# AdaLN block with a scan: one weight matrix laid out with its input features in partitions, its row norms summed on TensorE

## The chip, the cores and the metric

The kernel runs on one core of a Trainium2 chip. The metric is the device time of one execution in microseconds (us), as the median of several runs. The program is compiled from a hand-written order: each of the five engines (PE = TensorE, DVE = VectorE, ACT = ScalarE, POOL = GpSimd, SP = SyncE, which here only issues DMAs) works through its own queue strictly in order and waits on semaphores for the others.

## The reference, cut to what matters

```python
mod = (silu(c) @ wmod).reshape(2, 6, 1, 512)          # sa, ca, ga, sb, cb, gb
h = layernorm(x) * (1 + ca) + sa                      # x: 2 x 4096 x 512
xn = h / norm(h) * sqrt(512) * gamma
q, kv, a = split(einsum('bnd,ed->bne', xn, W_qkva), 3)   # W_qkva: 1536 x 512
a = sigmoid(a)
y_t = a_t * y_{t-1} + kv_t                            # scan along the 4096 rows
x = x + ga * (q * y)
h = layernorm(x) * (1 + cb) + sb
x = x + gb * fp4_linear(silu(fp4_linear(h, w_gate)) * fp4_linear(h, w_up), w_down)
```

`fp4_linear` quantizes both operands in blocks of 16. All inputs and the output are f32. Only the first product, with `W_qkva`, and what prepares it is touched here. To keep f32 accuracy the kernel splits each operand of that product into two f16 parts, "hi" and "lo", and sums three products (hi·hi, hi·lo, lo·hi). Every row of `W_qkva` times gamma is first scaled by the reciprocal of its norm, and the scale is multiplied back behind the product.

## The kernel before, in words

**Stages.** The first stage (attention) takes up about the first 580 us, the second (the feed-forward network) the rest. The attention stage is a loop over `slot` = 0 to 63 and three more. Slot `4*i + e` computes block `i` (512 rows of x) against group `e` (128 features of each of the three parts q, kv, a): `mix` issues 3 parts x 4 input chunks x 3 passes = 36 matmuls of 128x128 by 128x512. In slot 0 the block is cut into four quarters of 128 rows, so that each quarter can start when its own rows are there.

**What a slot needs.** (1) The rows of x: 128-row tile `g` is loaded (`norm_load`), its moments taken on DVE (`norm_moments`, `norm_stats`, two small POOL operations), centred and shifted on DVE (`norm_center`, `norm_shift`), squared on ACT with a sum (`norm_square`), turned into a reciprocal norm by two small POOL operations (`norm_gain`), scaled to f16 on ACT (`norm_hi`), its remainder formed on DVE (`norm_lo`), and both halves are transposed by a DMA on SP's queue into `xT`. Tiles 0 to 3 are prepared in `start`; tile `slot + 4` is finished in each slot, so slot 4 can begin when tile 7 has been transposed. (2) The weights of group `e`. Before, a piece of `W_qkva` arrives with its 128 *output* features in partitions. It is multiplied by gamma (DVE, L281), squared and summed on ACT (`square_qkva`, L285), its scale computed (`inverse_qkva`, a DVE operation and a POOL power, L288 and L289), split into hi (ACT or DVE, L308 and L310) and lo (DVE, L316), and transposed by a DMA on SP's queue (L324): twelve pieces, three for each group. Groups 0 and 1, and most of 2, are made in `start`, group 3 in slots 0 and 1. (3) The PSUM banks of two slots earlier read out.

**Behind each product**, one slot later: `gates` (ACT sigmoid), `scan` (DVE), `read_out` (DVE), `halves` (ACT copy, DMA transpose), then `joined` (ACT) and `residual` (POOL add, POOL's DMA).

**The opening** also computes the modulation rows on PE: `mod_spread(1, 0)` and `mod_spread(0, 0)` (each four f32 products, spread over all partitions, copied to `ca[0]` and `sa[0]`), `mod_rows` twice, and `mod_columns(2)` behind slot 0. Their weights `wmod` come in 256 KB loads.

**What sets the order.** `order = tc.manual_schedule(...)`: every engine's queue, SP's included, is the order of the Python calls. The SP queue carries all loads and all DMA transposes; a DMA reuses one of eight semaphores and therefore also waits for the DMA issued eight places earlier.

Of the kernel before, what the change touches and what calls it, by code (L numbers as in the profile page):

```python
# [6 lines left out]

# [36 lines left out]
def tile_adaln_block(  # L44
# [150 lines left out]
    wq = {divmod(n, 3): piece(2, n, 1) if n < 11 else piece(1, 2 * KC, 1) for n in range(12)}  # L195

    cT = atile([P, KC, B], F32, "cT")
    sc = atile([P, KC, B], F32, "sc")
    with nc.allow_non_contiguous_dma(reason="c is 4 KB"):
        for b in range(B):  # L200
            S.dma_start(cT[:, :, b], c[b].rearrange("(k p) -> p k", p=P))
# [4 lines left out]

    def load_part(e, part):
        S.dma_start(wq[e, part], w_qkva[part * D + e * P : part * D + (e + 1) * P, :])
# [61 lines left out]
    gam = ctile([P, D], F32, "gam", tag="mod_gb")  # L270
    wqT = atile([P, 2 * KC, 3 * D], F16, "wqT")
    us = atile([P, KC, 3], F32, "us")
    rs = atile([P, KC, 3], F32, "rs")
    gq = atile([P, KC, B], F32, "gq")

    def load_qkva(e):
        for part in (2, 1, 0):
            load_part(e, part)

    def gamma_qkva(e, part, engine=G):  # L280
        engine.tensor_tensor(wq[e, part], wq[e, part], gam, ALU.mult)  # L281

    def square_qkva(e, part):
        sq = work.tile([P, D], BF16, name="sq", tag="sq", bufs=1)
        A.activation(sq, wq[e, part], AF.Square, accum_out=us[:, e, part : part + 1])  # L285

    def inverse_qkva(e, a=0, b=3):
        V.tensor_scalar(rs[:, e, a:b], us[:, e, a:b], 1e-36, 2.0**-28, ALU.max, ALU.mult)  # L288
        G.tensor_tensor(rs[:, e, a:b], rs[:, e, a:b], mhalf[:, : b - a], ALU.pow)  # L289

    def scale_qkva(e):
        inverse_qkva(e)
        gain_qkva(e)

    def gain_qkva(e):
        V.tensor_scalar(
            us[:, e, :], us[:, e, :], 1e-36, 2.0**-28 / (XGAIN * XGAIN), ALU.max, ALU.mult
        )
        G.tensor_tensor(us[:, e, :], us[:, e, :], phalf[:, :3], ALU.pow)

    whl = {}

    def hi_qkva(e, part, on_act):
        w = wq[e, part]
        hl = whl[e, part] = new_hl()
        rsc = rs[:, e, part : part + 1]
        if on_act:
            A.activation(hl[:, 0, :], w, AF.Copy, scale=rsc)  # L308
        else:
            V.tensor_scalar(hl[:, 0, :], w, rsc, None, ALU.mult)  # L310

    def lo_qkva(e, part):
        w = wq[e, part]
        hl = whl.pop((e, part))
        r = part * KC + e
        V.scalar_tensor_tensor(  # L316
            out=hl[:, 1, :],
            in0=w,
            scalar=rs[:, e, part : part + 1],
            in1=hl[:, 0, :],  # L320
            op0=ALU.mult,
            op1=ALU.subtract,
        )
        S.dma_start_transpose(wqT[:, :, r * P : (r + 1) * P], flat(hl))  # L324
# [22 lines left out]
    def norm_shift(g):  # L347
        shift(xh[g], xstat.pop(g)[1], sa[g * P // N])
# [35 lines left out]
    def mix(i, xT, e):  # L384
        ps = [bank(3 * (e % 2) + j) for j in range(3)]
        width = P if i == 0 and e == 0 else TB
        for t in range(0, TB, width):
            for pp, part in zip(ps, PARTS):
                r = part * KC + e
                n = 0  # L390
                for k in range(KC):
                    for wp, xp in PASSES:
                        T.matmul(  # L393
                            pp[:, t : t + width],
                            wqT[:, wp * KC + k, r * P : (r + 1) * P],
                            xT[:, xp * KC + k, t : t + width],
                            start=n == 0,
                            stop=n == 3 * KC - 1,
                        )
                        n += 1  # L400
        return i, e, ps
# [245 lines left out]
    def start():  # L647
        a, b_, c_ = PARTS

        def load_mod_piece(s, k):  # L650
            S.dma_start(wm[s][:, k, :], wmod[k * P : (k + 1) * P, s * D : (s + 1) * D])

        load_mod(1, KC)
        norm_load(0)
        S.dma_start(gam, gamma.partition_broadcast(P))
        for k, then in enumerate((PARTS[0], PARTS[1], PARTS[2], None)):
            if then is None:
                norm_load(1)
            else:
                load_part(0, then)  # L660
            load_mod_piece(0, k)
# [3 lines left out]
        norm_load(KC)  # L665
        pc = mod_spread(1, 0)
        ps = mod_spread(0, 0)
        r1 = mod_rows(1)
        r0 = mod_rows(0)

        norm_moments(0)
        norm_stats(0)
        gamma_qkva(0, a, V)
        A.activation(ca[0], pc, AF.Copy, bias=1.0)
        square_qkva(0, a)
        gamma_qkva(0, b_, V)
        square_qkva(0, b_)
        inverse_qkva(0, a, a + 1)
        norm_center(0)
        gamma_qkva(0, c_, V)  # L680
        inverse_qkva(0, b_, b_ + 1)
        hi_qkva(0, a, True)
        square_qkva(0, c_)
        lo_qkva(0, a)
        inverse_qkva(0, c_, c_ + 1)
        hi_qkva(0, b_, True)
        norm_moments(1)
        norm_stats(1)
        lo_qkva(0, b_)
        A.copy(sa[0], ps)  # L690
        norm_center(1)
        hi_qkva(0, c_, True)
        norm_shift(0)
        norm_square(0)
        lo_qkva(0, c_)
        norm_gain(0, G)
        norm_shift(1)
        norm_square(1)
        norm_hi(0)
        norm_moments(2)  # L700
        norm_moments(3)
        norm_gain(1, G)
        norm_stats(2)
        norm_hi(1)
        norm_stats(3)
        norm_lo(0, xT)
        load_mod_piece(2, 0)
        norm_center(2)
        norm_shift(2)
        norm_square(2)  # L710
        norm_lo(1, xT)
        load_mod_piece(2, 1)
        load_part(2, a)
        norm_gain(2, G)
        norm_center(3)
        norm_shift(3)
        norm_square(3)
        norm_gain(3, G)
        norm_hi(2)
        gamma_qkva(1, a, V)  # L720
        norm_lo(2, xT)
        load_mod_piece(2, 2)
        load_part(2, b_)
        norm_hi(3)
        gamma_qkva(1, b_, V)
        square_qkva(1, a)
        square_qkva(1, b_)
        norm_lo(3, xT)
        load_mod_piece(2, 3)
        load_part(2, c_)  # L730
        norm_load(KC + 1)
        inverse_qkva(1, b_, a + 1)
        gamma_qkva(1, c_, V)
        mod_store(*r1, tag="yh")
        square_qkva(1, c_)
        mod_store(*r0)
        hi_qkva(1, a, False)
        inverse_qkva(1, c_, c_ + 1)
        lo_qkva(1, a)
        hi_qkva(1, b_, True)  # L740
        norm_moments(KC)
        hi_qkva(1, c_, True)
        lo_qkva(1, b_)
        gamma_qkva(2, a, V)
        square_qkva(2, a)
        norm_stats(KC)
        lo_qkva(1, c_)
        norm_load(KC + 2)
        load_qkva(3)
        norm_center(KC)  # L750
        gamma_qkva(2, b_, V)
        square_qkva(2, b_)
# [3 lines left out]
        gamma_qkva(2, c_, V)  # L756
        square_qkva(2, c_)
        gain_qkva(0)
        norm_moments(KC + 1)
        inverse_qkva(2)  # L760
        norm_stats(KC + 1)
        for part in PARTS:
            hi_qkva(2, part, False)
            lo_qkva(2, part)
        gain_qkva(1)
        gain_qkva(2)

# [7 lines left out]
    with order:  # L775
        xT = new_xT()
        start()
        for slot in range(NS + 3):
# [9 lines left out]
            cur = mix(i, xT, e) if slot < NS else None  # L788
# [12 lines left out]
            if slot == 1:  # L801
                for part in PARTS:
                    square_qkva(3, part)
# [7 lines left out]
            if gate is not None:  # L811
                gate = read_out(*gate)
            if g < NT:
# [15 lines left out]
            if slot == 1:  # L829
                scale_qkva(3)  # L830
                for part in PARTS:
                    hi_qkva(3, part, False)
# [228 lines left out]
```

## Time and profile before

| | us |
|---|---|
| median of 3 runs | 1935.84 (1935.71 to 1936.38) |
| time of the profiled execution | 1934.53 |
| its span in the profile | 1932.8 |
| PE busy in the span | 1905.7 (99%) |
| DVE / ACT / POOL busy | 1605.6 / 991.0 / 415.2 |
| attention product L393, 2412 matmuls | 505.2 |
| feed-forward products L888 (two lines) and L935 | 487.7 + 487.7 + 465.8 |

The chain that ended last is PE for 87% of the span. A busy PE is a PE with a matmul in flight; a wait shows as idle time with what released it. The profile's `PEclk` is the TensorE clock that was granted, in shares of full speed. `L393 PE MATMUL mm<-xT,wqT` reads: line 393, engine PE, writes tile `mm`, reads `xT` and `wqT`.

### The profile page before, as it was taken

The page shows a single profiled execution, that of the slowest core. Times are in us where ns is not written, and L with a number is a line of the kernel's source. Part 1 is how long each engine was busy: PE and PEld are TensorE (multiplying, and loading weights), DVE is VectorE, ACT ScalarE, POOL GpSimd, SP SyncE. Part 2 cuts the span into 40 slices and gives each one's busy share as a digit, 9 for nine tenths or more (in the row PEclk, how much of TensorE's full clock was granted, in tenths as well). Part 3 has the DMA queues.
Part 4 walks back from the last instruction along what each step waited for, and adds up shares of the span by engine and source line. Part 5 has one row for each costly group of instructions (what it writes and reads, how often), then busy time and mean ns, then how long its engine had stood idle before and what let it go on. Part 6 is the DMA issues. An engine that isn't in the chain of part 4 may idle for free.

```text
span 1932.8 us, 25689 instructions
## 1 busy us (share of the span) xinstructions
PE 1905.7 (99%) x9220; PEld 899.6 (47%) x9220; DVE 1605.6 (83%) x2677; ACT 991.0 (51%) x1705; POOL 415.2 (21%) x597
## 2 busy tenths in 40 slices
PE   7899999999999999999999999999999999999999
PEld 4344444444444444444444444444444444444444
DVE  6777789999859988888888888878888888888875
ACT  4544467777755544444444444444544454444432
POOL 4544466666520100000000100001000000000000
PEclk9999999999999999999999999999999999999999
DMA  9787689999933444334433443344434333433343
GB/s 234 182 233 189 165 184 201 220 202 202 188 85 60 87 72 80 69 63 76 79 66 63 78 80 74 63 82 81 63 63 82 76 63 66 81 74 63 63 68 58
DMA packets 483201, 206.67 MB, mean 107 GB/s; under 512 B 439622, under 2 KB 440902, under 8 KB 483072
## 3 DMA queue, kind: packets, MB, share of 16 engines
q1 hardware_dynamic: 468624, 171.50, 41.8%
q0 software_dynamic: 14448, 33.52, 10.0%
q8 instruction: 72, 1.18, 0.3%
q14 instruction: 57, 0.47, 0.1%
HBM read 63.12 MB, written 33.58 MB: 50 GB/s over the span
## 4 chain that ended last, share of the span: by engine, by line
PE 87%; DVE 0%; issue 0%; ACT 0%; POOL 0%; ACTq 0%
PE mm L888 47%; PE sd L935 24%; PE mm L393 16%; ACT y L435 0%; DVE o L953 0%; DVE o L964 0%; DVE ld L172 0%; DVE st L153 0%; DVE hl L372 0%; DVE y L420 0%; DVE ld L166 0%; DVE hid L908 0%; ACT sig L405 0%; ACT sq L354 0%; DVE inv L100 0%
## 5 line engine op out<-in xcount | busy, mean ns | idle before, releaser
L888 PEld LDWEIGHTS <-x2T 128*128 128x128 f16 x4608 | 450.9, 98 | 469.4 <-issue 1.3
L393 PE MATMUL mm<-xT,wqT 128*128 128x512 f16 (+1 forms) x2412 | 505.2, 373 | 15.0 <-DMA xT<-hl 8.0
L888 PE MATMUL mm<-wuT,x2T 128*128 128x512 f16 (+1 forms) x2304 | 487.7, 361 | 1.0 <-DVE hid L908 1.0
L888 PE MATMUL mm<-wgT,x2T 128*128 128x512 f16 (+1 forms) x2304 | 487.7, 361 | 0.0
L935 PE MATMUL sd<-wdT,hT 128*128 128x512 f16 x2112 | 465.8, 379 | 0.0
L393 PEld LDWEIGHTS <-wqT 128*128 128x128 f16 x2412 | 231.9, 99 | 289.8 <-issue 22.0
L935 PEld LDWEIGHTS <-hT 128*128 128x128 f16 x2112 | 206.7, 98 | 242.7
L903 ACT ACTIVATE silu<-mm,u 128x512 f32<-128x512 f32 (+1 forms) x192 | 124.6, 650 | 285.7 <-PE mm L888 281.9
L908 DVE SCALAR_TENSOR_TENSOR hid<-mm,u,silu 128x512 f32<-128x512 f32 (+1 forms) x192 | 128.6, 673 | 139.8 <-PE mm L888 130.7
L590 POOL TENSOR_SCALAR rstd<-vs 128x1 f32<-128x1 f32 x64 | 14.9, 232 | 982.8 <-ACT sq L588 982.8
L143 ACT ACTIVATE u<-ud,rms 128x1 f32<-128x1 f32 x64 | 18.9, 295 | 278.3 <-DVE rms L139 278.3
L120 ACT ACTIVATE sle<-sl 128x512 f16<-128x512 f32 (+2 forms) x162 | 146.9, 907 | 0.0
L113 ACT ACTIVATE she<-sh 128x1408 bf16<-128x1408 bf16 (+1 forms) x128 | 128.3, 1003 | 4.1
L959 POOL DMA_DIRECT2D out_dram<-o x63 | 56.2, 892 | 270.2 <-DVE o L953 266.4
L411 DVE TENSOR_TENSOR_SCAN y<-sig,cy,mm 128x512 f32<-128x512 f32 x56 | 71.7, 1280 | 45.8 <-ACT sig L405 17.3
L427 ACT COPY yh<-y 128x1024 uint16<-128x1024 uint16 x64 | 66.9, 1046 | 79.6 <-DVE y L420 76.5
L122 DVE SCALAR_TENSOR_TENSOR xn<-hid,xn 128x1408 f32<-128x1408 f32 x64 | 103.6, 1619 | 3.7 <-ACT hid L116 3.7
L106 DVE TENSOR_TENSOR xn<-hid,inv 128x1408 f32<-128x1408 f32 x64 | 104.0, 1625 | 2.2
L125 DVE SCALAR_TENSOR_TENSOR hhl<-hid,xn 128x1408 f16<-128x1408 f32 x64 | 104.0, 1625 | 2.2
L147 DVE TENSOR_REDUCE amh<-hid 128x88 f32<-128x1408 f32 x64 | 103.7, 1620 | 2.2
L116 ACT ACTIVATE hid<-xn 128x1408 f32<-128x1408 f32 x64 | 88.2, 1378 | 30.9 <-DVE xn L106 30.9
L443 POOL TENSOR_TENSOR xr<-xr,y 128x512 f32<-128x512 f32 x64 | 81.4, 1271 | 54.1 <-ACT y L435 54.1
(113 smaller groups left out, 1912.0 us busy)
## 6 DMA issues: line engine op xcount, KB each, us to landing
ld<-out_dram SPq DMA_DIRECT2D x65, 256.0 KB, 2.9
xr<-in_L_attn_x_dram SPq DMA_DIRECT2D x64, 256.0 KB, 3.4
out_dram<-xr POOLq DMA_DIRECT2D x64, 256.0 KB, 3.9
out_dram<-o POOLq DMA_DIRECT2D x63, 256.0 KB, 3.9
ld<-in_L_ffn_w_gate_dram SPq DMA_DIRECT2D x22, 256.0 KB, 3.1
ld<-in_L_ffn_w_up_dram SPq DMA_DIRECT2D x22, 256.0 KB, 3.3
ld<-in_L_ffn_w_down_dram SPq DMA_DIRECT2D x16, 256.0 KB, 3.1
scratch<-in_L_wmod_dram SPq DMA_DIRECT2D x12, 256.0 KB, 4.2
```

The costliest lines, as they stand in the source:

```text
L106: V.tensor_tensor(blocks(xn), blocks(src), spread(inv, nb), ALU.mult)
L113: A.activation(blocks(she), spread(sh, nb), AF.Copy, scale=WPEAK)
L116: A.activation(a, xn, AF.Abs, scale=MAGIC)
L120: A.activation(blocks(sle), spread(sl, nb), AF.Copy, scale=WPEAK)
L122: V.scalar_tensor_tensor(out=xn, in0=a, scalar=FLOOR, in1=xn, op0=ALU.max, op1=ALU.add)
L125: V.scalar_tensor_tensor(out=nq, in0=a, scalar=FLOOR, in1=xn, op0=ALU.max, op1=ALU.subtract)
L147: V.tensor_reduce(am, src.rearrange("p (b k) -> p b k", k=QB), AX.X, ALU.max, apply_absolute_value=True)
L393: T.matmul(pp[:, t : t + width], wqT[:, wp * KC + k, r * P : (r + 1) * P], xT[:, xp * KC + k, t : t + width], start=n == 0, stop=n == 3 * ...
L888: T.matmul(pp[:, : n1 - n0], x2T[:, xp * KC + k, :], wt[:, wp * KC + k, n0:n1], start=n == 0, stop=n == 3 * KC - 1,)
L903: A.activation(sl[:, :w], pairs[j][0][:, :w], AF.Silu, scale=u[:, 0:1])
L908: V.scalar_tensor_tensor(out=hid[:, n0:n1], in0=pairs[j][1][:, : n1 - n0], scalar=u[:, 1:2], in1=sl[:, : n1 - n0], op0=ALU.mult, op1=ALU.mult,
L935: T.matmul(pd, hT[:, hp * IC + k, :], wdT[:, wd_chunk(wp, k), :], start=n == 0, stop=n == 3 * IC - 1,)
```

## The change: what it does

- The host hands `W_qkva` over rearranged as [group, input feature in a chunk, chunk, part x output feature]: input features lie in partitions, so no weight is transposed on the chip. The twelve loads of 256 KB become eight of 384 KB (`load_qkva`: two halves for each group).
- Gamma becomes one column per chunk (`gT`, 4-byte pieces) in place of a 128x512 spread tile.
- Row norms: `square_qkva` writes gamma-scaled squares (ACT, 128x384, bf16), `sum_qkva` sums them over partitions with 12 matmuls that have one moving column of ones.
- Scales: `inverse_qkva` (DVE, POOL power, then DVE writes a diagonal matrix `diag` and a reciprocal), `spread_qkva` (one matmul of ones by `diag`, 128x384 into PSUM).
- `scale_qkva` (DVE, weight times gamma times the spread scale, 128x384, four for each group), `hi_qkva` (ACT copy to f16, 128x768, two for each group), `lo_qkva` (DVE subtraction, 128x768, two for each group), straight into `wqT[e]`.
- `mix` becomes a generator that `start` steps by hand, so that other PE work can stand between the quarters of slot 0.
- `start` is rewritten. The load of x tile 7 now stands ahead of it. On PE the order is: sums of group 0, `mod_spread(1)`, spread of group 0, `mod_spread(0)`, `mod_rows` twice, quarter 0, sums of group 1, quarter 1, spread of group 1, quarters 2 and 3, sums of group 2. On DVE, group 0 is scaled and split ahead of the shift of x tile 0, and half of group 1 is scaled ahead of `norm_lo(3)`.
- In slot 1 PE issues: spread of group 2, two thirds of the slot's products, sums of group 3, the last third; then, ahead of slot 2, the spread of group 3. Groups 2 and 3 are scaled and split in slots 1 and 2.

```diff
-    wq = {divmod(n, 3): piece(2, n, 1) if n < 11 else piece(1, 2 * KC, 1) for n in range(12)}
+    def group(e):
+        j, n = (2, 3 * e) if e < 3 else (1, 2 * KC)
+        return piece(j, n, 3).rearrange("p (k f) -> p k f", k=KC)
+    wq = [group(e) for e in range(KC)]
...
-    def gamma_qkva(e, part, engine=G):
-        engine.tensor_tensor(wq[e, part], wq[e, part], gam, ALU.mult)
-    def square_qkva(e, part):
-        sq = work.tile([P, D], BF16, name="sq", tag="sq", bufs=1)
-        A.activation(sq, wq[e, part], AF.Square, accum_out=us[:, e, part : part + 1])
...
+    def square_qkva(e, k):
+        A.activation(wsq[:, k, :], wq[e][:, k, :], AF.Square, scale=gT[:, k : k + 1])
+    def sum_qkva(e, ps):
+        for part in range(3):
+            for k in range(KC):
+                T.matmul(ps[:, part : part + 1], wsq[:, k, part * P : (part + 1) * P],
+                    ones[:, :1], start=k == 0, stop=k == KC - 1)
+        return ps
+    def inverse_qkva(e, ps):
+        V.tensor_scalar(us[:, e, :], ps, 1e-36, 2.0**-28 / (XGAIN * XGAIN), ALU.max, ALU.mult)
+        G.tensor_tensor(rs[:, e, :], us[:, e, :], mhalf[:, :3], ALU.pow)
+        V.tensor_tensor(diag, ident.unsqueeze(1).to_broadcast([P, 3, P]),
+            rs[:, e, :].unsqueeze(2).to_broadcast([P, 3, P]), ALU.mult)
+        V.reciprocal(us[:, e, :], rs[:, e, :])
+    def spread_qkva(e, ps):
+        T.matmul(ps, ones, diag.rearrange("p a f -> p (a f)"), start=True, stop=True)
+        return ps
+    def scale_qkva(e, k, ps):
+        w = wq[e][:, k, :]
+        V.scalar_tensor_tensor(out=w, in0=w, scalar=gT[:, k : k + 1], in1=ps, op0=ALU.mult, op1=ALU.mult)
+    def hi_qkva(e, k):
+        hi, _ = parts_qkva(e, k)
+        A.copy(hi, wq[e][:, k : k + 2, :])
+    def lo_qkva(e, k):
+        hi, lo = parts_qkva(e, k)
+        V.tensor_tensor(lo, wq[e][:, k : k + 2, :], hi, ALU.subtract)
...
-        S.dma_start_transpose(wqT[:, :, r * P : (r + 1) * P], flat(hl))
...
+        for k in range(KC):
+            square_qkva(0, k)
+        w0 = sum_qkva(0, bank(3)[:, :3])
+        pc = mod_spread(1, 0)
+        inverse_qkva(0, w0)
+        b0 = spread_qkva(0, bank(4)[:, : 3 * P])
+        ps = mod_spread(0, 0)
+        r1 = mod_rows(1)
+        r0 = mod_rows(0)
...
+            if slot == 0:
+                start(turns)
+            elif slot == 1:
+                spread_ps = spread_qkva(2, side((P, 3 * P)))
+                step(turns, 2)
+            else:
+                step(turns, 3)
...
+                sum_ps = sum_qkva(3, side((P, 3)))
+                step(turns)
```

## The prediction

> **What bounds the kernel now.** First the busy time and PE's waits after 77 us, to see where anything can be won; then the windows of the opening and PE's timeline there.
>
> ```profile
> PE mm L393 <- DMA xT<-hl: 2.7, 1, 2.7
> PE mm L393 <- ACT y L435: 2.3, 1, 2.3
> PE mm L888 <- DVE hid L908: 1.0, 1, 1.0
> ```
>
> ```profile
> 24.30:43.10 18.80, 13.47 (x177) 13.08 (x177) 14.40 (x28) 10.01 (x24) 11.73 (x17) 0.91 1.06 207
> 43.10:59.00 15.90, 15.85 (x74) 6.90 (x73) 12.78 (x29) 6.60 (x16) 7.10 (x10) 1.00 0.83 183
> 59.00:76.90 17.90, 10.57 (x37) 4.11 (x37) 14.66 (x28) 9.40 (x18) 9.59 (x15) 0.81 0.74 160
> 76.90:100.00 23.10, 23.08 (x107) 10.47 (x108) 15.61 (x27) 12.18 (x22) 12.80 (x18) 1.00 0.91 214
> ```
>
> The first three lines are all of PE's waits from 77 us on (total, times, longest): the first is the wait that ends at 76.92, and only 3.3 us follow in 1850. The next four are windows: length, then busy PE, weight loads, DVE, ACT, POOL, the granted clock, DMA. From 76.9 us PE is full (23.08 of 23.10); between 59 and 76.9 it works 10.57 of 17.90 us, at 0.81 of the clock, while DVE is 82% busy. So whatever moves the start of slot 4, now 76.92, moves the end one for one, and nothing else in the change moves it: from slot 4 on each engine has the same work. PE's timeline shows what comes before:
>
> ```profile
> 25.63 2.17 PE L393 MATMUL mm<-xT,wqT 128*128 128x128 f16 x36 [1.25 <-DMA xT<-hl]
> 28.54 2.17 PE L393 MATMUL mm<-xT,wqT 128*128 128x128 f16 x36 [0.74 <-DMA xT<-hl]
> 33.63 2.91 PE L393 MATMUL mm<-xT,wqT 128*128 128x128 f16 x36 [2.92 <-DMA xT<-hl]
> 36.96 2.78 PE L393 MATMUL mm<-xT,wqT 128*128 128x128 f16 x36 [0.42 <-DMA xT<-hl]
> 39.57 3.69 PE L240 MATMUL sd<-sc,scratch 128*128 128x2 f32 x32
> 43.12 15.91 PE L393 MATMUL mm<-xT,wqT 128*128 128x512 f16 x72
> 63.69 10.54 PE L393 MATMUL mm<-xT,wqT 128*128 128x512 f16 x36 [4.66 <-DMA wqT<-hl]
> ```
>
> The four quarters of slot 0 each wait for their x tile; slots 1 and 2 run back to back; slot 3 waits 4.66 us for the weight transposes of group 3 and then runs at half clock; slot 4 waits for x tile 7. Behind the two late waits stands the DVE queue (tile 7's `norm_lo` runs at 71.90).
>
> **What the change removes.** Twelve weight transposes, 1.23 us of SP's queue each, and their landing (4.8 us median): the 4.66 us wait goes. But SP bounds nothing else, and DVE saves next to nothing. The groups of the first 77 us (count, then busy total and mean ns of one):
>
> ```profile
> L316 DVE SCALAR_TENSOR_TENSOR hl<-scratch,rs,hl 128x512 f16<-128x512 f32 x12 | 8.9, 745 | 0.8 <-ACT hl L308 0.5
> L281 DVE TENSOR_TENSOR scratch<-scratch,gam 128x512 f32<-128x512 f32 x12 | 8.1, 687 | 2.5 <-DMA scratch<-in_L_attn_W_qkva_dram 2.5
> L285 ACT ACTIVATE sq<-scratch 128x512 bf16<-128x512 f32 x12 | 7.5, 626 | 3.4 <-DVE scratch L281 1.9 <-DVE rs L288 0.6 <-DVE us L296 0.5
> L310 DVE TENSOR_SCALAR hl<-scratch,rs 128x512 f16<-128x512 f32 x7 | 3.4, 483 | 2.9 <-POOL rs L289 2.9
> ```
>
> Before: 8.9 + 8.1 + 3.4 + 11 small operations of 0.16 = 22.2 us. After: 16 scalings of 128x384 (0.75 for 512 elements by L316, three quarters of it 0.56; taken 0.62 for the fixed part; ends 0.48 by L310 and 0.75), 8 subtractions of 128x768 (0.69 for 512 by L281, half as many again 1.03; taken 0.96; ends 0.69 and 1.22 by L411's scan), 4 diagonals of 0.55 (three quarters of 0.69 and a little; ends 0.16 and 0.69), 8 small: 21.2 us.
>
> **What it adds.** On PE 48 one-column sums and 4 spreads. A sum: 0.06 (a 128x128 product, 2.17/36) to 0.23 (two records of L240, 3.69/16); I take 0.1 and 1.2 us for twelve. A spread 0.25 (between 0.06 and the 0.56 record of L221). All are in PE's queue ahead of matmuls, and each has ACT in front (four squares at 0.44 to 0.52, from L285's 0.63 less a quarter; ends 0.17, 0.63) and DVE, POOL (0.86, L299) and DVE behind: a round trip that none of the old steps made. I chain the engines' queues in their new order, with those rows, 2.75 us from a transpose's issue to landing (22.86 to 25.6), POOL's small pairs 0.43 + 0.78. The same chaining of the old queues ends with slot 4 at 77.2, against 76.92; it puts slot 1 at 40.7, against 43.1, as it misses the loads in front of transposes.
>
> 1. *Opening.* Ahead of the second half of group 0 now stand x tile 7 (moved to the head of SP's queue), gamma's 512 pieces (like one `cT` load) and its own 768 KB: 1.0 MB. The trace has 1.3 MB landed at 9.43; scaled from 3.5 us, 8.2, taken 8.8 (ends 7.3, 9.8). Two squares 9.8, sums 10.8. Only then `mod_spread(1)`, whose loads come later anyway: four f32 products. Warm one is 1.12 (13.70: four records 2.37), cold 1.67 (8 records 6.70). Taken 1.25: 15.8; the spread, behind it in PE's queue, 16.0; `mod_spread(0)` 21.0 (17.4 before).
> 2. *Tile 0.* Its shift is queued on DVE behind group 0 (four scalings, centring, two subtractions: 20.7) and needs `mod_spread(0)`: 21.1 to 21.8. Copy 0.58, square 0.82, POOL 1.21, hi 0.72: 25.3. `norm_lo(0)` stands behind tile 1's shift, which waits for POOL: 27.2. Landed 30.0; before 25.6. **+4.4.** `mod_rows` on PE end at 28.05, hidden by that; the identity that POOL and DVE now build is hidden by the 10.8 of step 1 (POOL did nothing until 10.44).
> 3. *Tiles 1 to 3* land at 33.2, 37.7, 44.2. Before `norm_lo(3)` on DVE now wait the diagonal of group 1 and two scalings. Its POOL power stands behind tile 3's gain (37.7): 38.6; diagonal 39.2; spread 39.5, and the third quarter waits behind it though tile 2 is there at 37.7; scalings 40.6; `norm_lo(3)` 41.4; landed 44.2, against 36.9. Slot 0 ends 46.4, against 39.7. **+6.7.**
> 4. Sums of group 2 1.2, `mod_columns` 3.7, spread 0.25: slot 1 at 51.5, against 43.1. **+8.4.** On DVE tile 4's shift waits behind the diagonal of group 2 (49.3).
> 5. *Slot 1.* Two thirds, 5.2, to 56.7. The sums of group 3 need squares that stand on ACT behind tile 5's square, the sigmoid and tile 5's hi (58.3): 60.1, sums 61.0; PE waits 2.1. Last third 63.6. Then the spread of group 3 needs DVE: gq, moments, read-out, two subtractions of group 2 (62 to 65.8), 0.17, POOL 0.86, diagonal 0.55: 67.5. PE waits 3.9. Slot 2 begins 67.75, where the old one began at 50.9.
> 6. Slots 2 and 3, 7.78 each (36 x 0.216): 83.4. DVE's iteration (group 3's scalings and subtractions, tile 6, to 79.2), square 80.0, sigmoid 80.6, scan, moments, read-out, `norm_lo(7)` 83.9, landed 86.7: slot 4 at 86.7, **+9.8**.
>
> I add 0.7 for the loads now standing between the x transposes, the sort of thing in which the chaining of the old queues was early: slot 4 at 87.4, +10.5. The profiled run took 1934.53, 1.3 under the median, to which I add: 1935.84 + 10.5 = **1946.3**.
>
> *Ends.* All new operations at cheap values and cold f32 products none: slot 4 at 81.7; loads 1.5 us earlier and POOL's pairs at 0.3 + 0.6 too: 77.7. All dear, loads 1 us later, f32 at 1.5: 93.9.
>
> *Clock.* The gaps before (59.03 to 63.69) gave slot 3 10.54 us in place of 7.78. The new gaps of 2.1 and 3.9 us in slot 1 can do that to slot 2, +2.8: 83.4 becomes 86.2, hidden by tile 7 at 86.7; without that cover it costs 2.8.
> The Trainium skill (TensorE: Matmul & The Clock Gate, "What's actually happening") says the array starts at half clock and is released only after a busy window of about 3.4 us, the windows running freely. The first row above (1.67 against 1.12 us) agrees, and it speaks against this change: PE now starts real work near 9.4 us, not 4.9. By the rule all of `mod_spread(1)` is cold, 6.7 us, and the sum grows by some 1.7 us as an estimate; by the row's mean of 1.25 it is as above.
>
> **Rivals.**
> - *Faster.* The transposes were what mattered: slot 3's wait (4.66), its half clock (2.76) and tile 7's 2.69 vanish, and slot 1 begins at 43.1 as before: slot 4 at 66.8, 1925.7. For it: the longest late wait names `wqT`. Against: it needs slot 0 to end no later than 39.7, and PE's queue now has sums and spreads of later groups in it. It decides from tile 3 landing at 36.9 or sooner with slots 2 and 3 back to back; slot 4 before 76.9 is the dividing line.
> - *Small loss.* The new operations are cheap, DVE catches up in slots 1 to 3: slot 4 at 79.5, +2.6, 1938.4. For: DVE's bound is only 82% busy. Against: the round trips are waits, not work.
> - *Large loss.* Cold clock through the opening, dear operations, no cover for half-clock slots: 93.9, +17, 1952.8.
>
> **How the numbers follow.** The forecast (slot 4 5 to 14 us later) 0.70, small loss 0.12, faster 0.09, large loss 0.09. Own range of the forecast 1941 to 1950; with the ends for 8 in 10: 1939 to 1952. About 0.2%, 3.9 us, is what a measurement here can tell from no change. Slower by more: 0.70 + 0.09 + nearly half of the small loss, 0.84; within: 0.07; faster: 0.09.
>
> **What would show it.** In the profile after: quarter 0 of L409 at about 30 (step 2); quarter 2 released by PE's spread L322 and DVE, not by `xT` (3); slot 1 near 51 (4); PE waiting inside slot 1 for ACT L294 and before slot 2 for DVE L313 (5); slot 4 at 87, released by `xT` (6). If slot 2 follows slot 1 without a gap, step 5 is wrong; slot 4 before 77 makes the whole forecast wrong.

## The result, and the profile after

The changed kernel takes **1946.46 us** (median of 4 runs, 1945.89 to 1946.77) against 1935.84 (also 4 runs, 1935.71 to 1936.38): ratio 1.0054, 95% interval 1.0037 to 1.0071. It is slower by 10.6 us. Its profiled execution took 1946.33 us, its span is 1944.2, the granted clock 0.993 (before 0.996).

Lines of PE's timeline of the changed kernel (start, length, work, wait and its releaser), from the first sums to slot 8; L409 is the product that was L393, L299 the sums, L322 the spread, L235 the f32 products of `mod_spread`:

```profile
8.72 0.40 PE L299 MATMUL mm<-ones,scratch 128*128 128x1 bf16 x9 [0.32 <-ACT scratch L294]
9.31 5.83 PE L235 MATMUL sd<-scratch,sc 128*128 128x512 f32 x8 [0.20 <-DVE us L309]
15.15 3.60 PE L235 MATMUL sd<-scratch,sc 128*128 128x512 f32 x8
28.31 2.17 PE L409 MATMUL mm<-xT,wqT 128*128 128x128 f16 x36 [2.60 <-DMA xT<-hl]
36.55 0.50 PE L322 MATMUL mm<-scratch,ones 128*128 128x384 bf16 x1 [0.78 <-DVE scratch L313]
36.85 4.05 PE L409 MATMUL mm<-xT,wqT 128*128 128x128 f16 x36
41.69 2.17 PE L409 MATMUL mm<-xT,wqT 128*128 128x128 f16 x36 [0.80 <-DMA xT<-hl]
43.70 0.44 PE L299 MATMUL sd<-ones,scratch 128*128 128x1 bf16 x12
47.74 7.03 PE L409 MATMUL mm<-xT,wqT 128*128 128x512 f16 x24
56.15 0.18 PE L299 MATMUL sd<-ones,scratch 128*128 128x1 bf16 x1 [1.39 <-ACT scratch L294]
64.75 0.42 PE L322 MATMUL sd<-scratch,ones 128*128 128x384 bf16 x1 [2.40 <-DVE scratch L313]
64.96 17.35 PE L409 MATMUL mm<-xT,wqT 128*128 128x512 f16 x72
84.56 40.70 PE L409 MATMUL mm<-xT,wqT 128*128 128x512 f16 x180 [2.25 <-ACT y L451]
```

The weight transposes' wait is gone: slots 2 and 3 run back to back. But quarter 0 starts at 28.31 instead of 25.63, quarter 2 stands behind the spread of group 1, and slot 1 has two waits of its own, one for the squares of group 3 (ACT), one for its diagonal (DVE). Slot 4 starts at 84.56, **7.64 us** later than before. The releaser named for slot 4 had long been done: x tile 7's transposition was issued at 80.37 and landed at 84.5. Its line in SP's queue:

```profile
80.37 1.28 SPq L392 DMA_TRANSPOSE xT<-hl  x1
```

PE's waits from 77 us on (total, times, longest), which were 2.7, 2.3 and 1.0 before:

```profile
PE mm L409 <- DMA xT<-hl: 3.8, 2, 2.9
PE mm L409 <- ACT y L451: 2.3, 1, 2.3
PE mm L905 <- DVE hid L925: 1.1, 1, 1.1
```

From slot 4 to the last product before took 1851.05 us, after 1854.79: another **3.74 us**. Of these, 1.69 lie in slots 4 to 8 (40.70 for 180 matmuls, where before needed 39.01), 0.63 in a wait at 253 us that grew from 2.31 to 2.94, 0.90 in a wait for an x tile at 382 us that the kernel before did not have, the rest in several places. 7.64 + 3.74 = 11.4 of the 11.8 us between the two profiled executions. These are single executions, and that of the kernel before was 1.3 us below its median: the medians, 10.6 us apart, leave 3.0 us for the part behind slot 4.

The new operations, as groups of the first 85 us (count, then busy total and mean ns of one):

```profile
L340 DVE TENSOR_TENSOR wqT<-scratch,wqT 128x768 f16<-128x768 f32 x8 | 7.4, 951 | 0.0
L327 DVE SCALAR_TENSOR_TENSOR scratch<-scratch,gT,mm 128x384 f32<-128x384 f32 x8 | 4.5, 608 | 4.2 <-PE mm L322 4.2
L313 DVE TENSOR_TENSOR scratch<-ident,rs 128x384 bf16<-128x384 bf16 x4 | 2.2, 558 | 6.1 <-POOL rs L312 6.1
L299 PE MATMUL sd<-ones,scratch 128*128 128x1 bf16 x24 | 1.4, 166 | 2.4 <-ACT scratch L294 2.4
```

DVE's work on the weights is a little less than the 22.2 us before: 4.5 and 4.4 (a second group of eight scalings), 7.4, 2.2 and 1.3 of small ones, 19.8 in all. New are the idle times: DVE waits 6.1 us for POOL's powers and 4.2 for PE's spreads.

### The profile page after: what moved, and what is told of

Its sections match the earlier page's. It is cut to its first block, busy times and chain, and to the rows that moved or that the text cites. A ratio compares the mean times of both kernels' runs of the same rounds, so it can differ in the third digit from the quotient of the medians.

```text
span 1944.2 us, 25727 instructions
## 1 busy us (share of the span) xinstructions
PE 1912.6 (98%) x9272; PEld 903.9 (46%) x9272; DVE 1604.1 (83%) x2673; ACT 993.8 (51%) x1700; POOL 404.7 (21%) x592
## 4 chain that ended last, share of the span: by engine, by line
PE 83%; DVE 1%; DMA 1%; issue 1%; ACT 0%; POOL 0%; SPq 0%; ACTq 0%; POOLq 0%; DVEq 0%
PE mm L905 45%; PE sd L952 23%; PE mm L409 14%; DMA xT<-hl 0%; DMA xr<-in_L_attn_x_dram 0%; POOL xr L459 0%; DMA ld<-in_L_ffn_w_up_dram 0%; DVE y L436 0%; DMA out_dram<-xr 0%; POOL out_dram L461 0%; DVE xn L123 0%; DVE ld L173 0%; DVE xn L107 0%; DVE hid L925 0%; ACT yh L443 0%
## 5 line engine op out<-in xcount | busy, mean ns | idle before, releaser
L409 PE MATMUL mm<-xT,wqT 128*128 128x512 f16 (+1 forms) x2412 | 510.8, 376 | 11.7 <-DMA xT<-hl 9.4
L409 PEld LDWEIGHTS <-wqT 128*128 128x128 f16 x2412 | 234.2, 100 | 289.1 <-issue 28.7
L427 DVE TENSOR_TENSOR_SCAN y<-sig,cy,mm 128x512 f32<-128x512 f32 x56 | 71.6, 1279 | 48.9 <-ACT sig L421 18.5
```

The lines of the kernel that those rows point to most:

```text
L409: T.matmul(pp[:, t : t + width], wqT[e][:, wp, k, part, :], xT[:, xp * KC + k, t : t + width], start=n == 0, stop=n == 3 * KC - 1,)
```

## The experiments

Times in us; "slot 4" is the start of its first product, "rest" from there to the last product, both in the run's profiled execution; the median is of all its runs. The ratio is to runs of the kernel before that were made beside each run, with medians of 1935.66 to 1936.18.

Each row has one profile. Up to slot 1 the changed kernel, e1, e9 and e11 are the same code, and their slot 1 started at 47.74, 53.10, 48.11 and 50.59: a difference of some us in that column shows no effect of an edit. x tile 7 landed at 84.5 to 85.6 in all four, so that slot 4, where no added products stand in front of it, is much steadier.

| run | what | slot 1 | slot 2 | slot 4 | rest | median | ratio to before (95%) |
|---|---|---|---|---|---|---|---|
| before | | 43.12 | 50.89 | 76.92 | 1851.1 | 1935.84 | 1 |
| after | | 47.74 | 64.96 | 84.56 | 1854.8 | 1946.46 | 1.0037 to 1.0071 |
| e1 | two fillings | 53.10 | 67.43 | 87.28 | 1850.3 | 1944.58 | 1.0029 to 1.0059 |
| e2 | no norms, groups 1 to 3 | 45.77 | 53.54 | 77.19 | 1854.2 | 1939.60 | 1.0009 to 1.0028 |
| e3 | opening reordered | 45.21 | 61.53 | 81.05 | 1854.3 | 1941.84 | 1.0019 to 1.0041 |
| e4 | all reordered | 46.02 | 56.74 | 74.39 | 1858.0 | 1936.91 | 0.9995 to 1.0014 |
| e6 | e4 again | 45.52 | 56.11 | 73.91 | 1855.1 | 1936.00 | one run |
| e7 | e4, row loads later | 45.27 | 55.55 | 73.66 | 1854.3 | 1935.49 | 0.9989 to 1.0008 |
| e8 | e7, tighter | 45.20 | 54.82 | 72.05 | 1852.4 | **1931.80** | 0.9971 to 0.9989 |
| e10 | e8 with fillings | 45.43 | 55.74 | 71.64 | 1852.1 | **1930.72** | 0.9969 to 0.9989 |
| e5 | group 3 forward | 50.84 | 61.35 | 82.03 | 1855.6 | 1943.35 | 1.0023 to 1.0053 |
| e12 | group 1 backward | 51.76 | 65.27 | 84.96 | 1855.1 | 1946.12 | 1.0037 to 1.0067 |
| e9 | ten products, slot 4 | 48.11 | 64.96 | 86.51 | 1853.7 | 1946.89 | 1.0043 to 1.0073 |
| e11 | five products, slot 4 | 50.59 | 65.70 | 85.42 | 1851.5 | 1944.15 | 1.0029 to 1.0063 |

The theory at the start: the loss is waiting, made by the order of the queues (squares, sums, DVE, POOL, DVE, PE, DVE for each group, in front of x tiles and slots), plus a halved clock behind long gaps. The rival: the new operations' own work.

### e2: without the norms of groups 1 to 3

```diff
     def square_qkva(e, k):
+        if e:
+            return
     def sum_qkva(e, ps):
+        if e:
+            return None
     def inverse_qkva(e, ps):
+        if e:
+            return
     def spread_qkva(e, ps):
+        if e:
+            return flat1
```

> The changed kernel without the row norms of groups 1 to 3: no squares, sums, power, diagonal and spread there; their scalings multiply by gamma and by ones kept in SBUF. Group 0 and the order of all that is left stay. Theory 'round trips': what is lost between 28 and 85 us is the waiting for PE, DVE, POOL, DVE, PE of these groups inside the queues. The wait of quarter 2 for the spread, the waits of 1.39 and 2.40 us in slot 1 and the sums go; slot 4 at 78 to 79.5, 5 to 6.5 us earlier; time 1940 to 1941.5. Rival 'work': DVE is the bound, and only its own work counts, 3 times 0.17 + 0.56 + 0.17 = 2.7 us: slot 4 at 81.9, time 1943.8. Rival 'opening': the loss is made before quarter 0 and the rest is hidden: no more than 1 us, 1945.5 or above.

Slot 4 came at 77.19, 7.4 us earlier, a little more than 'round trips' had said; DVE's own work, 2.7, is far too little, and 'opening' falls too: quarter 0 came at 27.83, nearly as late as in the changed kernel. So the round trips, their work on all engines included (ScalarE's squares too), carry nearly all of the loss up to slot 4; waiting and work are told apart by e4, which keeps all the work. The time fell by 6.9, to a little less than the expected range.

### e3: only the opening in another order

`inverse_qkva` is cut in two, `power_qkva` (DVE, POOL) and `diag_qkva` (DVE), so that other work can stand between them; this serves all reordered kernels.

```diff
-        load_qkva(0)
-        norm_load(0)
         load_mod(1, KC)
+        load_qkva(0)
+        norm_load(0)
         load_mod(0, KC)
...
+        pc = mod_spread(1, 0)
         for k in range(KC):
             square_qkva(0, k)
         w0 = sum_qkva(0, bank(3)[:, :3])
-        pc = mod_spread(1, 0)
-        inverse_qkva(0, w0)
-        b0 = spread_qkva(0, bank(4)[:, : 3 * P])
         ps = mod_spread(0, 0)
+        power_qkva(0, w0)
+        norm_center(0)
+        diag_qkva(0)
+        b0 = spread_qkva(0, bank(4)[:, : 3 * P])
...
+        norm_shift(0, ps)
+        norm_square(0)
...
+        norm_lo(0, xT)
+        norm_shift(1)
+        lo_qkva(0, 0)
+        lo_qkva(0, 2)
```

> The changed kernel with only its opening put in another order, every operation kept: the loads of the modulation weights first, those of group 0 between them, tile 7's last; on TensorE mod_spread(1) ahead of the sums of group 0; on DVE tile 0 ahead of tile 1 and its low part ahead of group 0's. Theory 'order': quarter 0 at 23 to 25 us rather than 28.3, slot 0's end 3 to 4 us earlier (about 40), but slot 4 only 1.5 to 2.5 us earlier, since from slot 1 on DVE's queue decides: slot 4 at 82 to 83, time 1944 to 1945. Rival 'volume': the loads of group 0 and the f32 products at half clock set quarter 0 whatever the order: quarter 0 not before 27.5, time 1945.8 or above. Rival 'one for one': nothing behind quarter 0 hides a gain: slot 4 at 80 to 81, time 1942.5.

PE's timeline of e3 (its product is L415, its spread L328):

```profile
23.10 2.17 PE L415 MATMUL mm<-xT,wqT 128*128 128x128 f16 x36
27.66 2.17 PE L415 MATMUL mm<-xT,wqT 128*128 128x128 f16 x36 [1.14 <-DMA xT<-hl]
33.58 0.37 PE L328 MATMUL mm<-scratch,ones 128*128 128x384 bf16 x1 [3.74 <-DVE scratch L319]
81.05 9.19 PE L415 MATMUL mm<-xT,wqT 128*128 128x512 f16 x34 [2.36 <-ACT y L457]
```

Quarter 0 starts at 23.1, 5.2 us earlier, sooner than in the kernel before: neither the loads nor the f32 products hold it, the order does, and 'volume' falls. Of the 5.2 the spread of group 1, still ahead of quarter 2, takes back a part (PE now waits 3.74 for it, 0.78 in the changed kernel); slot 1 gains 2.5 and slot 4 3.5. My 'order' was right in the cause and too small in the gain: slot 4 and the time (1941.84, 4.6 less) are nearer to 'one for one'. The 3.5 here and the 7.4 of e2 are more than the 7.64 that the change lost: either edit saves part of the same waiting, and the two can't be added.

### e4 and e6: the same operations, all in another order

The opening of e3; the squares, sums and powers of a group a tile or more ahead of its diagonal; `norm_lo(3)` ahead of half of group 1's scalings; group 2 scaled in slot 0's iteration, group 3 in slot 1's; in slot 3 tile 7 ahead of the scan. The core of it:

```diff
+        w1 = sum_qkva(1, bank(5)[:, :3])
         step(first, 3)
...
+        power_qkva(1, w1)
+        norm_gain(2, G)
+        norm_center(3)
+        norm_hi(2)
+        diag_qkva(1)
+        b1 = spread_qkva(1, bank(3)[:, : 3 * P])
+        step(first, 3)
...
+            if slot == 0:
+                power_qkva(3, sum_ps)
+                for k in range(0, KC, 2):
+                    scale_qkva(2, k, spread_ps)
+                    scale_qkva(2, k + 1, spread_ps)
+                    hi_qkva(2, k)
...
+            if slot in (3,):
+                norm_lo(g, nxT)
             if gate is not None:
                 gate = scan(*gate)
```

> The same layout and the same new operations, each as often as in the changed kernel, in another order throughout: the opening of the run above; squares, sums, powers and diagonals of each group issued a tile or more before they are needed, so that no engine waits for the round trip; the scalings of groups 2 and 3 a slot earlier; tile 7's low part ahead of slot 3's scan. Theory 'order': the queues chained with the durations measured in the changed kernel give slot 1 at 41.5, slot 4 at 70.3; with half-clock stretches on the path up to 75. Time 1929 to 1934, faster than the kernel before. Rival 'work': the new operations on DVE and PE cost what the change lost, whatever the order: slot 4 at 80 or later, 1942 or above.

Slot 4 started at 74.39, 10.2 us earlier than in the changed kernel with every operation still done: the rival 'work' falls. But the time came out at 1936.9, not 1929 to 1934: after slot 4 this profile, of a run of 1939.41, lost 7 us against before. PE's timeline and SP's queue of e4:

```profile
74.39 31.24 PE L415 MATMUL mm<-xT,wqT 128*128 128x512 f16 x144 [1.96 <-ACT cy L436]
108.94 9.63 PE L415 MATMUL mm<-xT,wqT 128*128 128x512 f16 x36 [3.31 <-DMA xT<-hl]
```

```profile
94.69 4.62 SPq L451 DMA_TRANSPOSE yt<-yh  x1
99.36 0.57 SPq L227 DMA_DIRECT2D scratch<-in_L_wmod_dram  x1
...
101.97 3.06 SPq L398 DMA_TRANSPOSE xT<-hl  x1
```

Slot 8 waits 3.31 us for x tile 11, and then runs at half clock for a while (9.63 for 7.78). Tile 11's transposition spent 3.06 us in SP's queue, behind loads that a transposition of 4.62 us had put off; e7's lines below show 1.29 and 1.23 at the same places.

Run e6 was the same kernel once more:

> The reordered kernel of the run e4 once more, unchanged, as a look at how its profile varies: in the one profile so far slot 4 started at 74.39, 2.5 us earlier than in the kernel before, and slot 8 waited 3.31 us for x tile 11, whose transposition took from 101.97 to 108.8. Theory 'collision by chance': another execution has slot 8's wait below 1.5 us and a time near 1935. Theory 'systematic': the wait is there again, 2.5 to 4 us, as the same loads are always in front of that transposition.

It waited 1.65 us at slot 8 and took 1936.00. The shorter wait is not chance in the tile: x tile 11 landed 34.50 us after the start of slot 4 in e4 and 34.53 in e6. In e6 the clock was halved in slot 4 itself, which took 9.45 us instead of 7.77, so that PE came to slot 8 1.7 us later and had that much less to wait. The traces speak for 'systematic', though the wait was below its 2.5 to 4.

### e7: two loads moved from slot 5 to slot 12

```diff
-            if slot == KC + 1:
+            if slot == 3 * KC:
                 ca[1] = mod_load(1, 1, "mod_c1")
```

> The reordered kernel of e4 with one more edit: the two loads of broadcast modulation rows (512 KB together) that SP issues in slot 5 are issued in slot 12; they are needed only from slot 27 on. Theory 'collision': in e4 the transposition of y in slot 6 took 4.62 us on SP's queue, as the loads of slot 5 were still running, and x tile 11, two places behind it, landed 6.9 us after its issue: slot 8 waited 3.31 us, and a half-clock stretch of 3.4 us followed. Without these loads slot 8 starts within 1 us of slot 7's end, and the time falls by 3 to 5 us against that profile: median 1932 to 1935. Rival 'pace': the chain of a tile through ScalarE, DVE and SP takes more than a slot (7.77 us) whatever is loaded: slot 8 still waits 2 us or more, median 1936 to 1937.

SP's queue of e7 at the same place:

```profile
94.01 1.23 SPq L451 DMA_TRANSPOSE yt<-yh  x1
...
100.74 1.29 SPq L398 DMA_TRANSPOSE xT<-hl  x1
```

x tile 11 landed 32.33 us after the start of slot 4, 2.2 sooner than in e4 and e6, and the wait of slot 8 is gone, as 'collision' said. Part of that is the clock again: slots 4 to 8 took 40.70 here, with a halved stretch, and e8 below, with the same loads moved and no such stretch, has the tile at 32.58 and waits 1.47. The median fell by 1.4 only (1935.49), just outside of its range; the intervals of e4 and e7 overlap.

### e8: the order tightened

```diff
         norm_center(3)
+        for k in range(KC):
+            square_qkva(2, k)
         norm_hi(2)
...
+        w2 = sum_qkva(2, bank(5)[:, :3])
         scale_qkva(1, 1, b1)
...
+                sum_ps = sum_qkva(3, bank(5)[:, :3])
+                spread_ps = spread_qkva(2, side((P, 3 * P)))
                 cols = mod_columns(2)
-                sum_ps = sum_qkva(3, bank(5)[:, :3])
-                spread_ps = spread_qkva(2, side((P, 3 * P)))
```

> The kernel of e7 with the order ahead of slot 1 tightened once more: the squares and sums of groups 2 and 3 a tile earlier (DVE waited 2.62 and 2.54 us for these sums in e4), the rows of the modulation stored earlier, the spread of group 2 ahead of mod_columns. Every operation is still done once. Theory 'order': the chained queues give slot 4 3.5 us earlier than e7's, 70 to 72, and the time falls by as much, to 1929 to 1932. Rival 'given back': from slot 4 on the stream of x tiles cannot come earlier, so that what slot 4 gains is lost in waits of PE for x tiles in slots 5 to 10, and the time stays within 1 us of e7's.

PE's timeline of e8:

```profile
24.49 2.17 PE L415 MATMUL mm<-xT,wqT 128*128 128x128 f16 x36
35.56 5.85 PE L415 MATMUL mm<-xT,wqT 128*128 128x128 f16 x72 [1.59 <-DMA xT<-hl]
45.20 9.62 PE L415 MATMUL mm<-xT,wqT 128*128 128x512 f16 x36
54.82 15.70 PE L415 MATMUL mm<-xT,wqT 128*128 128x512 f16 x72
72.05 31.24 PE L415 MATMUL mm<-xT,wqT 128*128 128x512 f16 x144 [1.52 <-ACT cy L436]
104.76 5.56 PE L415 MATMUL mm<-xT,wqT 128*128 128x512 f16 x25 [1.47 <-DMA xT<-hl]
```

Slots 1 to 3 follow each other without a wait, slot 4 starts at 72.05, and the median is **1931.80, 4.4 us below the kernel before** (1936.18 beside it) and 14.7 below the changed kernel. Slot 8 gives 1.5 back, so 'given back' holds for that much. In this profile the clock was never halved behind slot 4, in that of the kernel before once (1.69); in how many of the ten runs that was so isn't known.

### e5: group 3's squares, sums and diagonal forward

```diff
         w2 = sum_qkva(2, side((P, 3)))
+        for k in range(KC):
+            square_qkva(3, k)
...
+                sum_ps = sum_qkva(3, bank(5)[:, :3])
                 spread_ps = spread_qkva(2, side((P, 3 * P)))
-                step(turns, 2)
+                step(turns, 3)
...
+                power_qkva(3, sum_ps)
             if slot in (1, 2):
...
+            if slot == 1:
+                diag_qkva(3)
```

> The changed kernel with group 3's share moved forward, everything else as it is: its squares on ScalarE right behind those of group 2, its sums ahead of slot 1 on TensorE, its power ahead of group 2's scalings, its diagonal behind them. The two waits of PE that the trace names in slot 1, 1.39 us for the squares and 2.40 us for the diagonal, have no cause any more. Theory 'cover' (step 6 of the prediction: tile 7 sets slot 4): slot 2 starts 4 to 6 us earlier (59 to 61 rather than 64.96), but slot 4 only 0.5 to 1.5 us earlier, 83 to 84, with a longer wait for x tile 7 in front of it; time 1945 to 1946. Rival 'the named waits are the loss': slot 4 moves with slot 2, to 79 to 80.5, and the time to 1941 to 1942.

PE's timeline of e5, the spread of group 3 (no wait) and slot 4:

```profile
61.19 0.33 PE L328 MATMUL sd<-scratch,ones 128*128 128x384 bf16 x1
82.03 8.31 PE L415 MATMUL mm<-xT,wqT 128*128 128x512 f16 x27 [4.32 <-ACT y L457]
```

Slot 2 came 3.6 us earlier, slot 4 2.5: between the two theories. Tile 7 sets slot 4, as 'cover' says (the wait in front of it grew to 4.32), but it doesn't hide all: DVE's timeline of the changed kernel shows `norm_lo(7)` (L388) behind the scan of slot 2 (L427), which waits for PE.

```profile
77.14 1.22 DVE L427 TENSOR_TENSOR_SCAN y<-sig,mm 128x512 f32<-128x512 f32 x1 [1.16 <-PE mm L409]
...
79.56 0.74 DVE L388 SCALAR_TENSOR_TENSOR hl<-ld,rn,hl 128x512 f16<-128x512 f32 x1
```

### e12: group 1's round trip behind tile 3

```diff
-        inverse_qkva(1, w1)
-        b1 = spread_qkva(1, bank(3)[:, : 3 * P])
-        step(first, 3)
...
+        norm_lo(3, xT)
+        inverse_qkva(1, w1)
+        step(first, 3)
+        b1 = spread_qkva(1, bank(3)[:, : 3 * P])
...
-        norm_lo(3, xT)
```

> The changed kernel with step 3 of the prediction undone alone: tile 3's low part is queued on DVE ahead of the diagonal and the scalings of group 1, and on TensorE the spread of group 1 stands behind quarter 2 rather than ahead of it. Theory 'cover': quarter 2 waits for its x tile alone, quarter 3 lands 2 us or more earlier, slot 0 ends 1.5 to 2.5 us earlier (41.2 to 42.2 rather than 43.7), but slot 1 waits for group 1's scalings on DVE and starts within 0.7 us of 47.74, slot 4 likewise within 1 us of 84.56 or later; time 1945.8 to 1947.3. Rival 'chain': what slot 0 gains is passed on, slot 1 at 45.7, slot 4 at 82.5, time 1944.4.

Quarter 3 started 1.4 us earlier (40.27), slot 1 4.0 later (51.76): the squares of group 2 were late for PE now (waits of 2.1), and `mod_columns` ran partly at half clock (6.30 us instead of 3.71); the changed kernel's own slot 1 varies by as much. Slot 4 and the time are unchanged, as 'cover' said, though slot 1 was missed by far. Here a round trip put off was no better than one put in front; e8 issues it early.

### e1, e9, e10, e11: products that keep TensorE busy

```diff
+    def fill(n):
+        w = wqT[0][:, 0].rearrange("p k a f -> p (k a f)")
+        for _ in range(n):
+            T.matmul(bank(0), w[:, :P], w[:, :TB], start=True, stop=True)
...
                 inverse_qkva(3, sum_ps)
+                fill(9)
...
+                if slot == KC:
+                    fill(10)
                 step(turns, 3)
```

e1 has both calls, e9 the second alone, e11 the second with 5; e10 is e8 with `fill(6)` ahead of the spread of group 1 and `fill(5)` ahead of the sums of group 2.

> The changed kernel with 19 products added on TensorE whose result nobody reads: 9 of 128x512 f16 (1.95 us at 0.2165) ahead of the spread of group 3, where PE waits 2.40 us for DVE, and 10 (2.17 us) ahead of slot 4, where it waits 2.25 us. Theory 'clock': the half-clock window 85.3 to 88.7 follows from the gap of 82.3 to 84.6. Then slot 4 starts where it did (84.6 give or take 0.3), slots 2 and 3 take about 15.6 us rather than 17.35 (which makes the wait before slot 4 longer, not slot 4 earlier), and slots 4 to 8 take 39.0 rather than 40.7: 1.7 us less, 1944.8. Rival: the 1.7 us in slots 4 to 8 are waits for transfers or for PSUM, and the clock only goes with them: no change, 1946.5, or slower by the part of the products that the gaps don't cover (up to 0.5).

> The changed kernel with ten products of 128x512 f16 (2.17 us) whose result nobody reads, ahead of slot 4 alone; in e1 the products ahead of the spread of group 3 as well left a half-clock stretch of 13.65 us behind the opening and slot 4 at 87.3, so that it did not show the second gap by itself. Theory 'clock': slot 4 starts at 84.3 to 85 as in the changed kernel, no half-clock stretch follows, slots 4 to 8 take 42.47 rather than 44.16 (from slot 4's start to slot 9's), the time falls by 1.7: 1944.5 to 1945. Rival: the stretch comes whatever PE does there, or returns elsewhere: 1946 to 1946.8.

> As e9 with five products in place of ten ahead of slot 4. In e9 a product took 0.426 us, not the 0.2165 that it was priced at, so that the ten (4.26 us) put off slot 4 to 86.5, 1.95 later than in the changed kernel, which used up what the clock gave back; slots 4 to 8 did take 42.46. Five take 2.13 and fit into the gap of 2.25. Theory 'clock': slot 4 at 84.3 to 84.9, slot 9 42.5 later, no half-clock stretch between; time 1944.5 to 1945.2. Rival: it makes no difference to the time, 1946 to 1946.8, because the stretch comes back later in the run.

> The kernel of e8 with eleven such products in two gaps of slot 0, 6 ahead of the spread of group 1 (1.30 us in a gap of 1.70) and 5 ahead of the sums of group 2 (1.08 us in a gap of 1.59). In e8 the clock was halved from 28.7 to 38.9 and from 45.7 to 49.1: quarters 1 to 3 took 4.00 and 5.85 rather than 2.17 and 4.34 us, slot 1 9.62 rather than 7.78. Theory 'covered': with the clock up slot 1 starts 1 to 2 us earlier, slot 2 2 to 4 us earlier, but slot 4 waits for x tile 7, which DVE sets, and moves by less than 1 us; time 1931 to 1932. Rival 'clock on the path': slot 4 moves with slot 2, 69 to 70, and the time to 1929 to 1930. If the products come in the way instead (half clock doubles them), slot 4 is later than 72.5 and the time above 1932.5.

PE's timeline of e9, then of e11:

```profile
82.19 4.26 PE L422 MATMUL mm<-wqT 128*128 128x512 f16 x10
86.51 39.01 PE L409 MATMUL mm<-xT,wqT 128*128 128x512 f16 x180
```

```profile
82.93 2.11 PE L422 MATMUL mm<-wqT 128*128 128x512 f16 x5
85.42 39.01 PE L409 MATMUL mm<-xT,wqT 128*128 128x512 f16 x180 [0.38 <-PE mm L422]
```

Where PE is kept busy ahead of slot 4, slots 4 to 8 take 39.01 instead of 40.70, in e1, e9 and e11 alike: the 1.69 us are the clock's. Ten products were too many (0.426 each, not the 0.2165 they were priced at) and put slot 4 off by 1.95, which is why e9 gained nothing. With five slot 4 started at 85.42, 0.5 beyond its range, since x tile 7 landed at 85.33 only, and the time fell to 1944.15, 2.3 less, more than expected: in the profiled execution no halved stretch followed the wait at 252 us either, one of another 1.69 that the kernels before and after both have. One of its four runs still took 1946.80, and its interval overlaps that of the changed kernel: the 39.01 us carry the argument, not the time. e1's 1.9 has the same two sources; its slot 4 was late: nine products of 3.83 us stood in a gap of 2.40. That its clock was halved from 44.2 to 57.9 can't come from them, as the expectation of e9 has it: the first of them starts at 63.54. In e10 slots 1 and 2 did not come earlier, since the halved stretch moved to slot 1 (10.32 us); slot 4 came 0.4 earlier, as 'covered' had it, and the ratio to its own runs of the kernel before (0.9979) is that of e8 (0.9980).

## Why the prediction came out as it did

The total is right, 1946.46 for 1946.3, and so is the way in which slot 4 gets late. That the number fits so closely is luck: slot 4 came 2.8 us before the 87.4 of the sum, and what lies behind it took 3.0 us longer by the medians (3.74 by the two profiles), where the sum has nothing.

| step | predicted | measured |
|---|---|---|
| 1: sums of group 0 end, `mod_spread(0)` ends | 10.8, 21.0 | 9.1, 18.75 |
| 2: quarter 0 | 30.0 | 28.31 |
| 3: quarter 3 starts, slot 0 ends | 44.2, 46.4 | 41.69, 43.8 |
| 4: slot 1 | 51.5 | 47.74 (48.11, 50.59, 53.10 in e9, e11, e1) |
| 5: PE's waits in slot 1; slot 2 | 2.1 and 3.9; 67.75 | 1.39 (then three of 0.33) and 2.40; 64.96 |
| 6: tile 7's low part ends, the tile lands | 83.9, 86.7 | 80.30, 84.47 |
| 6: slot 4 | 86.7, with the addition 87.4 | 84.56 |
| from slot 4 on | as before | +3.74 |

- *Steps 1 to 6: the mechanism was right at each place named* (quarter 2 released by the spread and DVE, PE waiting for ACT L294 and DVE L313, slot 4 by tile 7), and the terms were too dear. Step 1: the sums of group 0 ended 1.7 sooner, its loads having landed at 7.52 rather than 8.8; the eight f32 products took 9.4 us for 10.0, the first four 5.83, mostly at half clock (it was granted in full from 13.67 us on; wholly cold they were put at 6.7), the other four 0.90 each. Step 4: twelve sums took 0.44, not 1.2. The round trips cost about what was assumed (square 0.60, power 0.87, diagonal 0.56, scaling 0.61, subtraction 0.95), so they stayed the main loss: e2 gives them, with their own work, 7.4 us of slot 4. Step 5 came out nearly right in length (17.2 us for 16.25) by two errors that offset each other: shorter waits, and products partly at half clock, 7.03 and 4.44 us for 5.2 and 2.6, which its sum doesn't have. In step 6, 67.75 and two slots of 7.78 make 83.3, not 83.4; nothing rests on it.
- *The addition of 0.7 for loads between the x transposes* was too small: tile 7 took 4.10 us from issue to landing, tiles 1 and 2 4.74 and 3.75, where the sum has 2.75. It doesn't show in slot 4, as DVE was done with tile 7's low part 3.6 us ahead of the sum.
- *Failed: "whatever moves the start of slot 4 moves the end one for one, and nothing else in the change moves it".* The rest took 3.74 more. 1.69 of it are shown to be the clock's (e1, e9, e11): the paragraph on the clock looked for halved slots only ahead of slot 4, where tile 7 covers, and not behind the wait for tile 7 itself. Of the remaining 2 us 1.5 are longer waits for x tiles at 253 and 382 us. The rest varies from one execution to the next (1858.0 in e4 and 1855.1 in e6, one and the same kernel), so that these waits need not come from the change; what decided them was not tried. The sentence also fails on the other side: e4 started slot 4 2.5 us earlier than before and gained nothing.
- *Clock, "hidden by tile 7 at 86.7":* slots 2 and 3 did take 17.35 instead of 15.6. The cover is partial, since tile 7 is queued on DVE behind slot 2's scan (e5: 2.5 of 3.6 us came through).
- *Rivals.* Small loss and faster fall on slot 4 (84.56, not 79.5 or 66.8); 'large' needed products that stay at half clock and sums of 0.23. What the faster rival wanted, slot 1 at 43.1 and no waits behind it, e8 comes near to with slot 1 at 45.20, and ends 4.4 us below the kernel before.

## What to carry to other kernels

A step that goes from one engine through three others and back costs little work and much waiting; what it cost here was decided by how early it was issued, not by what it computes: the same operations in another order were worth 14.7 us. And a late start is not passed on one for one: a wait of more than about 2 us in front of a stretch that fills TensorE can cost a halved clock as well, and a start that comes earlier can run into the next stream of tiles.

## What was not expected of the hardware

**Which waits halve the clock.** The granted clock changes only at the edges of fixed stretches of 3.41 us: between the first release and the end of the work the halved times of the 14 profiles last 3.41, 6.83, 10.24 or 13.65 us, and the full ones are multiples of 3.41 too. Windows laid on such stretches (length, then busy PE and other engines, the granted clock last but two), of the kernel before, of the changed kernel and of e11:

```profile
72.40:75.80 3.40, 1.83 (x9) 0.63 (x7) 2.12 (x7) 2.21 (x5) 2.68 (x5) 1.00 0.70 150
75.80:79.20 3.40, 2.28 (x11) 1.10 (x12) 3.40 (x6) 2.54 (x4) 2.29 (x4) 1.00 0.69 161
243.10:246.50 3.40, 1.09 (x6) 0.42 (x5) 1.92 (x4) 3.05 (x6) 2.72 (x5) 1.00 1.12 202
246.50:249.90 3.40, 3.40 (x9) 1.18 (x8) 2.87 (x6) 1.45 (x2) 2.94 (x5) 0.50 0.49 141
```

```profile
81.90:85.30 3.40, 1.15 (x6) 0.41 (x5) 2.16 (x4) 3.05 (x6) 2.11 (x4) 1.00 1.12 200
85.30:88.70 3.40, 3.40 (x10) 1.22 (x9) 2.60 (x5) 1.72 (x3) 2.60 (x4) 0.51 0.53 143
```

```profile
250.80:254.20 3.40, 1.41 (x7) 0.44 (x5) 1.88 (x3) 2.21 (x5) 2.94 (x6) 1.00 1.01 193
254.20:257.60 3.40, 2.64 (x13) 1.24 (x14) 3.37 (x7) 2.07 (x4) 2.58 (x3) 1.00 0.54 125
```

Before slot 4 the kernel before waited longer (2.69) than the changed one (2.25), but its wait fell over an edge: 1.83 and 2.28 us of work in the two stretches, and the clock stayed up. The changed kernel's fell into one stretch, 1.15 us of work, and the next was halved. Over the 14 profiles, between 50 and 400 us, each of 20 stretches at full clock with 0.98 to 1.97 us idle was followed by a full one, and each of 25 with 2.03 us or more by a halved one. Where the edges lie differs from one execution to the next: in the changed kernel, e1, e9 and e11, the same code up to there, the clock first came up at 13.67, 13.52, 14.13 and 15.24 us. So a wait of 2.25 us cost 1.69 us here and one of 2.69 us nothing. The Trainium skill (TensorE: Matmul & The Clock Gate, "What's actually happening") has the free-running window of 3413 ns, which agrees, and puts the return to half clock down to at least one idle window; here 2.03 us idle of 3.41 was enough.

**Busy is not active.** In e1 PE was busy for 13.50 of 13.50 us and the clock stayed halved nearly throughout; half of that is `mod_columns`, 32 f32 products with two moving columns, which took 6.97 us there and 3.71 in the changed kernel. There, too, the stretch from 44.40 to 47.80 was full of these products (busy 3.40 of 3.40 us, at the full clock) and the next, to 51.22, was halved. Why this is so was not tried. PE's timeline and a window of e1:

```profile
46.00 6.97 PE L254 MATMUL sd<-sc,scratch 128*128 128x2 f32 x32
```

```profile
44.00:57.50 13.50, 13.50 (x77) 10.57 (x75) 9.81 (x19) 4.33 (x10) 6.32 (x11) 0.51 0.44 139
```

**A product that starts and stops its own sum, again and again in one PSUM bank,** took 0.42 us at the full clock (4.26 for ten in e9, 2.11 for five in e11), where the kernel's own of the same shape take 0.217 (39.01 for 180). The added products also read both operands from one tile and use the same weights each time; which of these it is was not tried.
